# A two-layer kernel on one Trainium2 core: the first step of the forward transforms moves 128 columns (re, im) instead of 192, and the negative real part is made at the evacuation of four images

## Chip, core and metric

The kernel runs on one core of one Trainium2 chip. The metric is the device time of one execution in microseconds (us). Four executions of the kernel before gave 3290.41, 3295.86, 3288.34 and 3288.98 us, median 3289.7 us. The profile shown is of the execution that took 3290.41 us; its span from the first to the last instruction is 3288.7 us, so 1.7 us lie around the span.

Engines are called by their profile names: PE (TensorE, matmuls), PEld (its weight loads), DVE (VectorE), ACT (ScalarE), POOL (GpSimd), SP (SyncE, which here only issues DMAs).

## What is computed

The input is `x` of shape (4, 32, 128, 128) in float32, read as 4 batches of 32 images of 128 x 128. Layer 0 is a Fourier neural operator block with attention; layer 1 is causal attention and a mixture of eight experts over tokens. The change lies in layer 0 alone, and of layer 0 only the forward transforms matter here:

```python
def _spectral_conv(x, w2, oh, ow):
    w = w2[..., 0] + 1j * w2[..., 1]
    X = jnp.fft.rfft2(x, norm='forward')
    Xk = jnp.concatenate([X[:, :, :mh, :mw], X[:, :, -mh:, :mw]], axis=2)
    Yk = jnp.einsum('bixy,ioxy->boxy', Xk, w)
    ...
    return jnp.fft.irfft2(out, s=(oh, ow), norm='forward')
...
xn = _inorm(xa, norm1_w, norm1_b)
k = _fno_layer(xn, Kcw, Ksw, Hs, Ws)          # and q, v: one spectrum of xn serves all three
...                                            # attention over the 32 images, projection p
a = _inorm(p + xa, attn_w, attn_b)
an = _inorm(a, norm2_w, norm2_b)
m = _fno_layer(an, m0cw, m0sw, H, W, inner_norm=True, act=True)
m = _fno_layer(m, m1cw, m1sw, H, W, inner_norm=True, act=False)
out = _inorm(m, mon_w, mon_b) + a
```

Each batch needs three sets of 32 spectra: of the input images (for k, q and v), of the attention's output (first mixer layer) and of its GELU (second mixer layer). Only 64 rows of modes and 33 (or 17) columns of modes are kept, so a truncated transform by two matmuls does it.

## The kernel before

Layer 0 takes the first third of the execution, about 1130 us, layer 1 the rest. Layer 1 has its own hand-written order and is not touched. In layer 0 the program text gives the dependencies and the buffers, and a scheduler with a cost model of its own decides at build time in which order each engine gets its instructions. An edit of an instruction's size can therefore move instructions elsewhere in layer 0; the engines then run their queues strictly in that order.

**The forward transform** (`forward`, L265 to L281) works on groups of eight images (`GI = 8`).

- Step one, L272: for each image one matmul `pz[:, j] = image.T @ rows`. The image is the stationary operand (a 128 x 128 weight load), the constant `rows` is moved. `rows` has 192 columns: cos, -sin, -cos (64 each), so that the result holds the real part, the imaginary part and the negative real part. Two images share one PSUM tile `pz` of 2 x 192 floats; the tag "a" has two such banks, which other stages of layer 0 use as well (the `pv2` of the inverse transforms among them).
- Evacuation, L217 or L219: `evacuate` copies the tile to `z` in SBUF, 128 x 384 floats at once. A counter sends two calls of three to ACT and one to DVE. Four evacuations serve a group.
- Step two, L279 and L280: for each image two matmuls with `z` as stationary operand, accumulating in `px`: `z[:, :128]` (re, im) against the constant `c1`, then `z[:, 64:]` (im, -re) against `c2`. The moved operand has 99 columns (67 for the input images). Four images share a `px` tile; `take` is then called with it.

`forward` is called in three places, each four times per batch (four groups of eight images), 48 times in all:

- `spectra_of_images` (trace name of the moved image: x): `take` is `scaled`, L467 on DVE. Before step two `less_mean` (L472, L473, DVE) subtracts a mean from the first column of the real and of the negative real part of all eight images at once. Its results go out by DMA (`xd`, L485) and come back spread over partitions (`xb`, L696), and they feed `attention_weights` (L526 to L616), where the products `pa` and `pb` (L557 on DVE, L559 on POOL) go into the matmuls of L563.
- `spectra(0, q)`: `take` is `weighted`: a square on ACT (L791), two products on DVE (L792, L795), a sum on POOL (L798). In the same stretch of time DVE does `add_attention` (L768, 32 instructions a batch).
- `spectra(1, gl)` (image: g), likewise; at its end the weights by energy (L808, L812 on DVE, L814 on PE).

So per batch the order of the stages is: values by attention (L711 to L716, L661, L680), inverse transform with L746 and L748, `spectra(0)`, inverse transform with the GELU (L838 to L848), `spectra(1)` and the next batch's `spectra_of_images` side by side, the next batch's `attention_weights`, the last inverse transform (L899). L887 (ACT) and L894 (POOL, 2.4 us each) prepare the last stage and may be placed anywhere between the end of `spectra(1)` and L899. DMAs of SP are issued in order of its queue; in batch 0 this queue holds the two halves of `gd` and `gb` (L515, L517: weights written to DRAM and read back onto all partitions), `xd` and `xb`.

Of the kernel before, what the change touches and what calls it, by code (L numbers as in the profile page):

```python
# [7 lines left out]
F32 = mybir.dt.float32  # L8
AF = mybir.ActivationFunctionType
ALU = mybir.AluOpType  # L10
# [3 lines left out]
P = 128  # L14
# [4 lines left out]
GI = 8  # L19
# [16 lines left out]
def _constants():  # L36

    w = np.arange(P)
    kx = np.concatenate([np.arange(32), np.arange(-32, 0)])
    ky = np.arange(KY)  # L40
    th = 2 * np.pi / P
    c, s = np.cos(th * np.outer(w, kx)), np.sin(th * np.outer(w, kx))
    rows = np.concatenate([c, -s, -c], 1)
    inv_rows = np.concatenate([c.T, -s.T], 0)
    angle = th * np.outer(w, ky)
    cc, cs = np.cos(angle), np.sin(angle)

    cols1 = np.concatenate([cc[:, 32:33], cs, cc, -cs], 1) / NPIX
    cols2 = np.concatenate([0 * cc[:, :1], -cc, cs, cc], 1) / NPIX
    twice = np.where(ky == 0, 1.0, 2.0)[:, None]  # L50
    re, im = twice * cc.T, -twice * cs.T
    inv_cols = np.concatenate([re, im], 0)
    p = np.arange(P)
    same = (p[:, None] % 32 == np.arange(32)[None, :]).astype(np.float64)
    block = (p[:, None] // 32 == np.arange(4)[None, :]).astype(np.float64)

    eye = np.eye(32)
    comb = np.zeros((4, 32, 3, 32))
    comb[0, :, 0], comb[3, :, 0] = eye, -eye
    comb[1, :, 1], comb[2, :, 1] = eye, eye  # L60
    comb[:, :, 2] = -comb[:, :, 0]
    halves = np.concatenate([np.eye(64), np.eye(64)], 0)

    group = (p[:, None] // 4 == p[None, :] // 4) / (4.0 * NPIX / C * T)
    of_group = p[:, None] // 4 == np.arange(32)[None, :]
    by_p = np.concatenate(
        [rows, inv_rows, cols1, cols2, same, block, comb.reshape(P, 96), halves, group, of_group / 4],
        1,
    )
    return by_p.astype(np.float32), inv_cols.astype(np.float32)  # L70


NX = 1 + 3 * KY
NCONST = 192 + 128 + 2 * NX + 32 + 4 + 96 + 64 + P + 32
NM = KX * KY
NK = 13

# [25 lines left out]
def layer0(  # L103
    tc, x, kcw, qcw, vcw, pcw, m0cw, m1cw, mcol0, heads, small_row, by_p, inv_cols, dram, x1
):
    nc = tc.nc
    pools = [tc.tile_pool(name="l0_const", bufs=1), tc.tile_pool(name="l0_ps", bufs=2, space=PSUM)]
    pools.append(tc.tile_pool(name="l0_x", bufs=2))
    const, ps, images = (p.__enter__() for p in pools)
# [17 lines left out]
    def columns(n):  # L127
        at[0] += n
        return cst[:, at[0] - n : at[0]]

    rows = columns(192)
    inv = columns(128)
    cols1, cols2 = columns(NX), columns(NX)
    same, block = columns(32), columns(4)
# [75 lines left out]

    flip = [0]

    def evacuate(out, in_):

        flip[0] = (flip[0] + 1) % 3
        if flip[0]:
            nc.scalar.copy(out, in_)  # L217
        else:
            nc.vector.tensor_copy(out, in_)  # L219

    def per_image(name):
        return small.tile([P, T], F32, name=name, tag=name)
# [41 lines left out]
    def forward(images, c1, c2, take, change=None):  # L264


        n = c1.shape[1]
        z = grp.tile([P, GI, 192], F32, name="z", tag="z")
        for k in range(0, GI, 2):
            pz = ps.tile([P, 2, 192], F32, name="pz", tag="a")  # L270
            for j in range(2):
                nc.tensor.matmul(pz[:, j], images[k + j], rows, start=True, stop=True)  # L272
            evacuate(z[:, k : k + 2], pz)
        if change is not None:
            change(z)
        for k in range(0, GI, 4):
            px = ps.tile([P, 4, n], F32, name="px", tag="b")
            for j in range(4):
                nc.tensor.matmul(px[:, j], z[:, k + j, :P], c1, start=True, stop=False)  # L279
                nc.tensor.matmul(px[:, j], z[:, k + j, 64:], c2, start=False, stop=True)  # L280
            take(k, px)  # L281
# [343 lines left out]
    for b in range(B):  # L625
# [63 lines left out]
        for x0 in range(0, KX, NK):  # L689
# [3 lines left out]
            for i in range(4):  # L693
                xb = late.tile([P, 2, NK * KY], F32, name="xb", tag="xb")[:, :, :m]
                for r in range(2):
                    nc.sync.dma_start(  # L696
                        out=xb[:, r],
# [773 lines left out]
```

## Time and profile before

| part of the profiled execution | value |
|---|---|
| execution, span | 3290.41 us, 3288.7 us |
| ACT, POOL busy over the span | 2356.5 us (72%), 2140.0 us (65%) |
| L272, matmul records | 768 (two for each of 384 matmuls) |
| L279 and L280, matmul records | 768 each |
| L272's time in the 27 us from 473 to 500 us (`spectra(0)`, batch 1) | 12.35 us |
| the same in the 31 us from 558 to 589 us (mostly input images of batch 2) | 12.85 us |
| PE granted clock from 212 us to 327 us, and in the whole span | 1.00, 0.968 |

A float32 matmul of the program is shown as two records, each with its weight load. The time of one record contains its way through the array, so records of neighbouring matmuls overlap; what a matmul costs PE when others follow is the distance from start to start. In the groups, the columns are count, busy time in us, mean of one in ns, and the engine's idle time just before with what ended it. In the chain of waits, time is given to the work that everything after it waited for.

### The profile page before, as it was taken

How to read it: one execution, taken by the hardware profiler on the slowest of the kernel's cores; microseconds unless marked ns; L12 is line 12 of the kernel's file. 1: busy time of each engine (PE TensorE's matmuls, PEld its weight loads, DVE VectorE, ACT ScalarE, POOL GpSimd, SP SyncE). 2: the span in 40 equal slices, each digit the busy share in tenths (PEclk: the TensorE clock that was granted, in tenths of full speed). 3: DMA queues.
4: the chain of work that ended last, by engine and by line, in shares of the span. 5: the costliest groups of instructions: out<-in, count | busy, mean ns of one | idle time of the engine just before them, and what ended most of it. 6: DMA issues, size and time to landing. Idle time of an engine off the chain costs nothing.

```text
span 3288.7 us, 48731 instructions
## 1 busy us (share of the span) xinstructions
PE 3068.0 (93%) x17428; PEld 1494.7 (45%) x17428; DVE 2319.8 (71%) x5070; ACT 2356.5 (72%) x3205; POOL 2140.0 (65%) x1883
## 2 busy tenths in 40 slices
PE   6899899899898699999999999999999999999997
PEld 4378368458558533333333333333333334333333
DVE  6866776767677456777665767766777777677777
ACT  2334344354344289999999999998999999999992
POOL 1731641551460278868788787889877879888773
PEclk8999999999999689999999999999999999999998
DMA  4400410320230111010110000011100010101000
GB/s 108 118 21 5 117 48 1 78 91 1 32 111 1 52 39 26 1 33 7 27 33 20 14 20 14 7 26 26 26 20 14 14 33 20 33 1 26 14 13 13
DMA packets 148274, 107.17 MB, mean 33 GB/s; under 512 B 35358, under 2 KB 138881, under 8 KB 147425
## 3 DMA queue, kind: packets, MB, share of 16 engines
q1 hardware_dynamic: 131313, 98.22, 11.6%
q10 hardware_dynamic: 16720, 5.84, 0.7%
q8 instruction: 138, 2.26, 0.3%
q14 instruction: 103, 0.84, 0.1%
HBM read 67.26 MB, written 20.00 MB: 27 GB/s over the span
## 4 chain that ended last, share of the span: by engine, by line
PE 72%; POOL 10%; DVE 8%; ACT 4%; issue 3%; DMA 2%; ACTq 0%; POOLq 0%; DVEq 0%; SPq 0%
PE d L1282 25%; PE po L1301 13%; PE px L1180 6%; PE po L716 4%; PE pz L272 4%; PE four L294 3%; POOL e L1344 3%; PE pv L289 3%; POOL e L1343 3%; PE px L280 2%; PE px L279 2%; ACT r L1335 2%; PE n L1282 2%; POOL kx L1044 1%; PE sk L680 1%
## 5 line engine op out<-in xcount | busy, mean ns | idle before, releaser
L1282 PE MATMUL d<-qe,ke 32*128 32x512 f32 (+7 forms) x3456 | 1167.6, 603 | 20.8 <-ACT r L1335 20.2
L1340 DVE TENSOR_TENSOR r<-n,r 128x1024 f32<-128x1024 f32 (+1 forms) x1056 | 958.2, 949 | 302.8 <-ACT r L1347 169.5
L1282 PE MATMUL n<-qf,kf 32*128 32x512 f32 (+7 forms) x3456 | 1159.9, 602 | 0.0
L1343 POOL TENSOR_TENSOR e<-r 128x512 f32<-128x512 f32 x528 | 672.8, 1274 | 318.2 <-DVE r L1340 277.6
L1335 ACT ACTIVATE r<-d 128x1024 f32<-128x1024 f32 (+1 forms) x1056 | 822.7, 805 | 70.3 <-PE n L1282 60.0
L1347 ACT ACTIVATE r<-r 128x1536 f32<-128x1536 f32 x528 | 783.4, 1484 | 16.8
L1344 POOL TENSOR_TENSOR e<-e,r 128x512 f32<-128x512 f32 x528 | 672.4, 1273 | 41.4
L1282 PEld LDWEIGHTS d<-qe,ke 32*128 32x128 f32 (+1 forms) x3456 | 352.4, 185 | 701.8 <-issue 243.4
L1301 PE MATMUL po<-e,kx 128*128 128x512 f32 (+3 forms) x1152 | 596.3, 606 | 10.5 <-POOL e L1356 10.5
L1184 DVE SCALAR_TENSOR_TENSOR xc<-px,wgt,xc 128x128 f32<-128x128 f32 x1024 | 358.2, 350 | 212.0 <-PE px L1180 179.4
L1351 ACT ACTIVATE e<-e 128x512 f32<-128x512 f32 x528 | 325.9, 617 | 75.6 <-POOL e L1344 74.9
L1282 PEld LDWEIGHTS n<-qf,kf 32*128 32x128 f32 (+1 forms) x3456 | 350.9, 184 | 19.0 <-DVE r L1340 0.9
L1301 PEld LDWEIGHTS po<-e,kx 128*128 128x128 f32 x1152 | 176.2, 188 | 382.6 <-issue 298.4
L711 POOL TENSOR_TENSOR u<-xb,gb 128x858 f32<-128x858 f32 (+1 forms) x120 | 234.9, 1985 | 117.4 <-PE po L716 106.1
L798 POOL TENSOR_TENSOR spec<-spec,part 128x264 f32<-128x264 f32 x64 | 55.4, 866 | 392.2 <-DVE part L795 188.9
L1180 PE MATMUL px<-we,x2t 128*128 128x512 f32 x512 | 265.9, 605 | 7.0 <-DVE xc L1184 6.2
L713 DVE TENSOR_TENSOR u<-xw,gb 128x858 f32<-128x858 f32 (+1 forms) x200 | 208.5, 1093 | 50.5 <-PE po L716 34.9
L716 PE MATMUL po<-u,pr 128*32 128x429 f32 (+1 forms) x1280 | 187.0, 532 | 19.3 <-POOL u L711 8.7
L705 ACT COPY xw<-xb 128x429 f32<-128x429 f32 (+1 forms) x160 | 83.8, 527 | 127.9 <-DVE pa L557 68.6
L1180 PEld LDWEIGHTS px<-we,x2t 128*128 128x128 f32 x512 | 96.6, 194 | 121.4 <-issue 104.6
L217 ACT COPY z<-pz 128x384 f32<-128x384 f32 x127 | 60.7, 478 | 119.7 <-PE pz L272 119.3
L559 POOL TENSOR_TENSOR pb<-xm 128x1024 f32<-128x1024 f32 x48 | 90.6, 1912 | 83.3 <-ACT xm L493 73.9
(365 smaller groups left out, 3917.6 us busy)
## 6 DMA issues: line engine op xcount, KB each, us to landing
xb<-xd SPq DMA_DIRECT2D x128, 214.5 KB
xc<-x SPq DMA_DIRECT2D x31, 512.0 KB
x<-x SPq DMA_DIRECT2D x16, 512.0 KB
kf<-ks SPq DMA_DIRECT2D x64, 128.0 KB
qf<-qe SPq DMA_DIRECT2D x64, 128.0 KB
out<-xc SPq DMA_DIRECT2D x15, 512.0 KB
xb<-xd SPq DMA_DIRECT2D x32, 198.0 KB
gb<-gd SPq DMA_DIRECT2D x4, 1056.0 KB
```

The lines of the kernel that those rows point to most:

```text
L711: nc.gpsimd.tensor_tensor(u, xb, gk, ALU.mult)
L716: nc.tensor.matmul(po[32 * j : 32 * j + 32], pr[:, i, k], u[:, r], start=i == 0 and k == 0, stop=i == 3 and k == 1,)
L1180: nc.tensor.matmul(px, x2t[:, k * P : (k + 1) * P], we[:, e0 : e0 + 4], start=True, stop=True)
L1184: nc.vector.scalar_tensor_tensor(xc[:, k], px[:, e], wgt[:, k, e0 + e : e0 + e + 1], xc[:, k], ALU.mult, ALU.add)
L1282: nc.tensor.matmul(o, k, q, start=True, stop=True)
L1301: nc.tensor.matmul(sums[c, h][:, q0 : q0 + c1 - c0], kx[:, jb], e[:, c0:c1], start=jb == 0, stop=is_last and q0 > 2 * P, skip_group_check= ...
L1335: nc.scalar.activation(r[:, g], d, AF.Ln, scale=1.0 / DSCALE)
L1340: nc.vector.tensor_tensor(r[:, g], part, r[:, g], ALU.mult)
L1343: nc.gpsimd.tensor_tensor(e, r[:, 0], r[:, 1], ALU.add)
L1344: nc.gpsimd.tensor_tensor(e, e, r[:, 2], ALU.add)
L1347: nc.scalar.activation(r, r, AF.Exp, scale=-1.0)
L1351: nc.scalar.activation(e, e, AF.Exp)
```

## The change

`rows` loses its third block of 64 columns, and L272 moves 128 columns. A `pz` tile now holds four images x 128 columns (one whole PSUM bank) instead of two x 192. For each tile there are two evacuations: re and im of four images (128 x 512 floats), and re again with the factor -1 into the third block of `z` (128 x 256 floats). A group of eight images still has four evacuations and `z` holds the same numbers as before. `evacuate` gets a `sign` and becomes an ACT activation `Copy` with a scale, or a DVE `tensor_scalar` multiply, for all its callers (`v` and `yf` of the inverse transforms too, with 1.0).

```diff
-    rows = np.concatenate([c, -s, -c], 1)
+    rows = np.concatenate([c, -s], 1)
...
-NCONST = 192 + 128 + 2 * NX + 32 + 4 + 96 + 64 + P + 32
+NCONST = 128 + 128 + 2 * NX + 32 + 4 + 96 + 64 + P + 32
...
-    rows = columns(192)
+    rows = columns(128)
...
-    def evacuate(out, in_):
+    def evacuate(out, in_, sign=1.0):
 
         flip[0] = (flip[0] + 1) % 3
         if flip[0]:
-            nc.scalar.copy(out, in_)
+            nc.scalar.activation(out, in_, AF.Copy, scale=sign)
         else:
-            nc.vector.tensor_copy(out, in_)
+            nc.vector.tensor_scalar(out, in_, sign, None, ALU.mult)
...
         z = grp.tile([P, GI, 192], F32, name="z", tag="z")
-        for k in range(0, GI, 2):
-            pz = ps.tile([P, 2, 192], F32, name="pz", tag="a")
-            for j in range(2):
+        for k in range(0, GI, 4):
+            pz = ps.tile([P, 4, P], F32, name="pz", tag="a")
+            for j in range(4):
                 nc.tensor.matmul(pz[:, j], images[k + j], rows, start=True, stop=True)
-            evacuate(z[:, k : k + 2], pz)
+
+            evacuate(z[:, k : k + 4, :P], pz)
+            evacuate(z[:, k : k + 4, P:], pz[:, :, :64], -1.0)
```

The built program, compared with the one before, has the same number of instructions on every engine. The 192 evacuations of `z` are split as before, 127 on ACT and 65 on DVE. Around the forward transforms of layer 0 the scheduler orders instructions of PE, DVE and ACT differently. On POOL ten places differ: among L559 and L894 (the next batch's `pb` and the sums for the last stage). On SP one transfer moves: the second half of `gd` (L515) stands after the two `xd` of batch 0 (L485), and before them in the kernel before. With layer 1 the order begins to be the same again.

## The prediction

> **What bounds the kernel.** I read the page's busy table and slices first, then the chain of waits, then the groups by shape, last the timeline and the chain inside the forward stages.
>
> ```profile
> PE 3068.0 (93%) x17428; PEld 1494.7 (45%) x17428; DVE 2319.8 (71%) x5070; ACT 2356.5 (72%) x3205; POOL 2140.0 (65%) x1883
> PE   6899899899898699999999999999999999999997
> DVE  6866776767677456777665767766777777677777
> PE 72%; POOL 10%; DVE 8%; ACT 4%; issue 3%; DMA 2%; ACTq 0%; POOLq 0%; DVEq 0%; SPq 0%
> ```
>
> PE is the bound in layer 0 (slices 1 to 13 of 82 us) as in layer 1, and holds 72% of the chain. On the page the same chain gives L272 4%, about 130 us. So the changed matmuls lie on the path that sets the end, not beside it. The chain cut to 460 to 600 us confirms it: L272, L279 and L280 follow each other there, and where PE stops it is for an evacuation:
>
> ```profile
> 482.23 1.34 PE pz L272 x8
> 483.59 0.49 ACT z L217
> 484.12 1.57 PE pz L272 x8
> ```
>
> What one matmul costs is its distance to the next. Timeline of PE, three stretches (start, time from first start to last end, count), and one from layer 1:
>
> ```profile
> 49.57 0.39 PE L280 MATMUL px<-colg,z 128*128 128x67 f32 x2
> 49.79 0.39 PE L279 MATMUL px<-colg,z 128*128 128x67 f32 x2
> ...
> 212.72 1.47 PE L272 MATMUL pz<-cst,q 128*128 128x192 f32 x8
> 214.75 1.57 PE L272 MATMUL pz<-cst,q 128*128 128x192 f32 x8 [0.57 <-ACT z L217]
> ...
> 1217.56 0.61 PE L1120 MATMUL pa<-centre,att 128*128 128x129 f32 x4
> ```
>
> L272 with 192 columns: (1.47 - 0.326)/7 = 0.163 us a record (0.326 is its median time). L279 with 67 columns: (49.79 - 49.57)/2 = 0.11 us. L1120 has 129 columns and the same full weight load: (0.61 - 0.275)/3 = 0.112 us. So 67, 99 and 129 columns cost the same 0.112 us: below some 130 columns another limit holds, and 128 columns get no cheaper than that. The 0.57 us in brackets is PE waiting for a `pz` bank.
>
> **What the Trainium skill says.** "TensorE: Matmul & The Clock Gate", section "LDWEIGHTS (loading the stationary operand)", prices a weight load at columns/1.2 ns; for 128 columns that is 107 ns, an estimate from the page. The measured 112 ns agrees, so the floor is the weight load. "VectorE: DVE Perf Modes", section "Why PSUM operands drop a tier", says that float32 from PSUM runs at the lowest rate whatever the operation, so DVE's multiply should cost what its copy did; the trace has no multiply of such a size from PSUM. "PSUM — Partial Sum Buffer", section "PSUM bank collisions raise a hardware error", says that ACT and DVE may not read the same bank at once, reads against reads included. The trace agrees in effect: L791 (ACT) and L792 (DVE) read the same `px`, and L792 waits for L791:
>
> ```profile
> L792 DVE TENSOR_TENSOR spec<-px,mcw 128x264 f32<-128x264 f32 x64 | 27.5, 430 | 40.0 <-ACT sqx L791 38.7
> ```
>
> So the two evacuations of one new `pz` bank run one after the other, on two engines too; the built order of the changed kernel has these waits.
>
> **The change part by part.** Rows used:
>
> ```profile
> L272 PE MATMUL pz<-cst,x 128*128 128x192 f32 x256 | 53.9, 352 | 4.1 <-ACT z L217 3.0 <-DVE z L219 1.0
> L272 PE MATMUL pz<-cst,g 128*128 128x192 f32 x256 | 51.5, 338 | 3.2 <-ACT z L217 1.6 <-DVE z L219 1.6
> L272 PE MATMUL pz<-cst,q 128*128 128x192 f32 x256 | 49.3, 335 | 3.0 <-ACT z L217 2.3 <-DVE z L219 0.6
> L217 ACT COPY z<-pz 128x384 f32<-128x384 f32 x127 | 60.7, 478 | 119.7 <-PE pz L272 119.3
> L219 DVE COPY z<-pz 128x384 f32<-128x384 f32 x65 | 35.8, 550 | 17.2 <-PE pz L272 16.1 <-issue 0.7
> L683 ACT COPY q<-sk 128x512 f32<-128x512 f32 x32 | 18.8, 587 | 39.0 <-PE sk L680 38.8
> L559 POOL TENSOR_TENSOR pb<-xm 128x1024 f32<-128x1024 f32 x12 | 22.7, 1914 | 28.8 <-ACT xm L493 28.0 <-PE sp L563 0.7
> L894 POOL TENSOR_TENSOR x<-x,g 128x1024 f32<-128x1024 f32 x4 | 9.5, 2366 | 0.7 <-DVE pa L557 0.7
> ```
>
> (The last two are of the window 318 to 372 us, POOL alone.)
>
> *Matmuls removed from PE:* 768 records x (0.162 - 0.112) = 38.4 us. Almost all on the path, since PE is 94 to 100% busy in most of the windows of these stages.
>
> *Old stalls removed:* from start to start, 693 pairs of neighbouring L272 records took 26.5 us more than 693 x 0.162; with the steps to and from L279 it is 29 us, 0.6 us for each of the 48 groups of eight. They come from a bank of two images: it fills in 4 x 0.162 = 0.65 us, and its evacuation (0.48 or 0.55 us, plus some 0.16 us until the last matmul has ended and 0.1 us of handover) must be over when the bank after the next is wanted. In the new form a group uses two banks only, each once, so this wait mostly goes.
>
> *New stalls added:* step two of images 0 to 3 now needs both evacuations of the first bank. From rows: ACT costs (587 - 478)/128 = 0.85 ns a float, so 0.59 us for 512 and 0.37 us for 256; DVE, with the 690 ns of L1060's 512-float copy from PSUM, 0.69 and 0.41 us. In series 0.96 to 1.1 us. Timeline for a group: the last matmul of the bank is issued, ends 0.27 us later, handovers 0.1 us, evacuations 1.05 us: `z` is whole 1.42 us after the issue. PE meanwhile fills the second bank (8 x 0.112 = 0.9 us) and does one or two L279 (0.22 us each) that need only the first evacuation; then L280 waits 0.2 to 0.3 us, plus 0.1 us for a weight load that can't be hidden behind it. With DVE evacuations queued behind other DVE work (L768 at 0.35 us, four L748 at 0.87 us together) I take 0.5 us a group, 24 us. Bounds: 0.2 us (10 us), where the scheduler puts other matmuls there (it interleaves two groups in the stage of the input images), and 1.0 us (48 us), where each DVE evacuation waits for a run of L768 or L748. Net of old and new stalls: -5 us; bounds -19 and +19.
>
> *Evacuations:* as many, the same floats, the same split over the engines: ACT 0.59 + 0.37 against 2 x 0.478 us, DVE 0.69 + 0.41 against 2 x 0.55 us. ACT changes from COPY to ACTIVATE; the nearest rows with a fixed scale, L1335 from PSUM, 595 ns for 512 floats, and L683's copy, 587 ns, differ by 1%. I take 0; ends -1 and +2 us over all 288 calls, `v` and `yf` included, most of it off the path.
>
> *`spectra(0)`:* DVE was busy 25.4 of the 28 us from 212 to 240. PE's gain there (3.2 us a batch plus stalls) nearly meets DVE's spare 2.6 us; in the new order several L768 come later, after the stage, from batch 1 on. I charge 1 us a batch for L768 between the steps of the chain from L812 to L838: +4 us (0 to 8).
>
> *POOL in `attention_weights`:* after `xm`, POOL is the bound: 12 L559 x 1.91 + 4 L894 x 2.37 = 32.4 us of the 33.3 us from 327.2 to 360.5. For batch 2 the kernel before runs two L894 ahead of `xm` (584 and 587 us, POOL idle otherwise) and needs 592.1 to 622.8 = 30.7 us. In the new order all four come among the L559, each behind ACT's L887 too: 33.3 us, +2.6 us; for batch 3 three instead of two or so, +1.5 us. Together +4 us (0 to 8).
>
> *SP's queue in batch 0:* the second `gd` was issued at 67.5 us, ahead of the two `xd` (75.3 to 79.9 us, waiting for the last spectra). It now stands behind them, the `gb` that reads it back waits for it, and the `xb` queue up behind `gb`. The chain there runs through them: `xd` 13.2 us, then `xb` 15.9 us to 105 us, and ACT's L705 waits for it. So of batch 0's gain in the stage of the input images (about 4 us) I give back 2 us (0 to 5).
>
> *`NCONST`* is 64 columns smaller: one load at the start, nothing. Layer 1 keeps its order and its clock (PE 1.00 in most of it); its start moves as a whole.
>
> Sum: -38.4 - 5 + 4 + 4 + 2 = -33.4 us. Against the profiled execution (3290.4 us; the median, 3289.7 us, is 0.7 us lower) that is 3257 us.
>
> **Rivals.**
>
> - *Handover dominates:* new stalls 0.8 us a group (38 us), the rest as above with POOL and SP at +10 us: -38.4 + 9 + 10 = -19 us, 3271 us. For it: the two evacuations in series on a shared bank, DVE 90% busy in `spectra(0)`. Against: DVE is only half to two thirds busy in the other two stages.
> - *Stalls nearly vanish:* 0.2 us a group, side costs 2 us: -38.4 - 19 + 2 = -55 us, 3235 us. For it: half as many banks to hand over. Against: the serial reads.
> - *Slower:* one mechanism, the serial pair at the head of each group behind a full DVE queue. Before, a group paid 0.6 us of stalls and 0.8 us (16 x 0.05) for the third block; if L280 waits more than 1.4 us a group (1.2 us with the 10 us of side costs) the change loses. At 1.6 us: 77 - 29 - 38 + 10 = +20 us, 3310 us. It decides only if nearly every group meets a DVE backlog of over 1 us, which the 0.57 us waits of before (one bank behind two L748 runs) show only for the first group of a stage.
> - *No floor below 192:* if 128 columns cost 0.16 us too, little would change; L1120's 0.112 us speaks against it.
>
> **Numbers.** Likeliest 3257 us: chance 0.56, its own range 3245 to 3270. Handover 0.22, stalls vanish 0.11, slower 0.08, nothing left 0.03. A measurement of this kernel tells about 0.2% (6.6 us) from no change: faster by more 0.88, within 0.04, slower 0.08. The range reaches into the two faster-side rivals, to 3234 us (stalls gone) and 3282 us (stalls 1.0 us a group, side costs at 10 us).
>
> **What would show it.** Right: L272 records 0.112 us apart, its group about 40 us less busy; idle before L272 falls, idle before L279 and L280 rises from 1.1 us to about 20 us, released by z on ACT or DVE; the ACT row of z split into 0.59 and 0.37 us; layer 1 unchanged in length. Wrong: L272's distance above 0.13 us; waits of L280 over 1 us in most groups; the stage from `xm` to the last L559 longer by over 5 us in batches 2 and 3; `xb` of batch 0 landing later than 105 us.

## The result, and the profile after

The changed kernel takes 3280.74 us (median of 41 runs, 3271.29 to 3288.64) against 3289.04 us (62 runs on the same chip): ratio 0.997, 95% interval 0.9964 to 0.9977. It is faster, by 8 to 12 us; 33 were forecast. The profiled execution took 3277.85 us (span 3276.1 us, 12.6 us below that of before).

The page of the kernel after, first the busy table, then PE's slices, then the chain of waits by engine:

```profile
PE 3036.1 (93%) x17428; PEld 1461.9 (45%) x17428; DVE 2317.9 (71%) x5070; ACT 2353.3 (72%) x3205; POOL 2139.9 (65%) x1883
...
PE   6699898899898699999999999999999999999997
...
PE 65%; POOL 10%; DVE 6%; ACT 5%; issue 3%; DMA 1%; SPq 0%; POOLq 0%; DVEq 0%; ACTq 0%
```

PE does 32 us less, DVE and ACT the same to 3 us, and the end comes only 12.6 us earlier. PE's second slice (82 to 164 us) fell from 8 to 6 tenths, so a part of what PE saved came back as waiting in batch 0. The groups by shape (busy us, mean ns of one, then idle time before and what ended it):

```profile
L272 PE MATMUL pz<-cst,x 128*128 128x128 f32 x256 | 37.3, 291 | 5.2 <-ACT z L217 5.0
L272 PE MATMUL pz<-cst,g 128*128 128x128 f32 x256 | 36.0, 287 | 0.0
L272 PE MATMUL pz<-cst,q 128*128 128x128 f32 x256 | 31.8, 276 | 0.0
L281 PE MATMUL px<-cst,z 128*128 128x99 f32 x512 | 101.7, 281 | 4.7 <-ACT z L217 2.4 <-DVE z L219 0.9 <-DVE n_r_ve L236 0.5
L217 ACT ACTIVATE z<-pz 128x512 f32<-128x512 f32 x63 | 37.6, 596 | 76.1 <-PE pz L272 74.7 <-issue 1.3
L217 ACT ACTIVATE z<-pz 128x256 f32<-128x256 f32 x64 | 24.3, 379 | 26.5 <-DVE z L219 26.5
L219 DVE TENSOR_SCALAR z<-pz 128x512 f32<-128x512 f32 x33 | 22.5, 682 | 3.8 <-PE pz L272 3.1 <-issue 0.7
```

Lines after L275 stand two lower than before (L279 is L281, L515 is L517, L696 is L698), and lower again in the experiments, which have a helper more. The last three rows show the new serial pair: over all 64 calls, ACT's copy of 256 floats stood 26.5 us for DVE's read of the same bank.

Where did the rest go? The starts of the same steps in both traces show it. In batch 0 the stage of the input images ended 1.2 us earlier than before, but the first L718 (`po`) started at 133.99 us instead of 119.98. When batch 1's first transform starts, the kernel is still 9.2 us late; from there to the last L901 (batches 1 to 3) it gains 21.6 us, and from there to the end both take 2164.8 to 2164.9 us. My sum, split the same way, had 8 us gained in batch 0 and 25.5 in the others: 17 of the missing 21 us of this execution are lost in batch 0.

SP's queue there, kernel before (start, time, issue, count):

```profile
58.04 1.35 SPq L517 DMA_DIRECT2D gb<-gd  x2
67.46 0.33 SPq L515 DMA_DIRECT2D gd<-g  x1
75.25 4.61 SPq L485 DMA_DIRECT2D xd<-xx  x2
80.76 2.33 SPq L517 DMA_DIRECT2D gb<-gd  x2
85.13 23.39 SPq L696 DMA_DIRECT2D xb<-xd  x10
```

and the kernel after:

```profile
61.16 1.36 SPq L519 DMA_DIRECT2D gb<-gd  x2
74.02 8.47 SPq L487 DMA_DIRECT2D xd<-xx  x2
82.58 2.65 SPq L517 DMA_DIRECT2D gd<-g  x1
91.58 1.27 SPq L519 DMA_DIRECT2D gb<-gd  x2
92.96 26.94 SPq L698 DMA_DIRECT2D xb<-xd  x10
```

The second `gd` now goes out 15.1 us later, behind both `xd`. SP stands 6.4 us (85.23 to 91.58) until it has landed, then issues the second pair of `gb`, 10.8 us later than before, and every `xb` is behind it. The first pair of `gb` is late as well, by 3.1 us, and the two `xd` hold SP for 8.47 us instead of 4.61. ACT and DVE in the kernel after show who is caught:

```profile
115.04 0.52 ACT L707 COPY xw<-xb 128x429 f32<-128x429 f32 x1 [38.05 <-DMA xb<-xd]
117.06 0.58 ACT L573 COPY spt<-sp 128x512 f32<-128x512 f32 x1
```

```profile
123.33 0.68 DVE L595 TENSOR_REDUCE mx<-sc 64x16 f32<-64x512 f32 x1 [20.56 <-PE sc L584]
```

`spt` could have run at 104 us, when its last L565 was done. It stands on ACT behind a `xw` that waits for `xb`, and the softmax behind `spt`: DVE waits 20.56 us (5.32 before). This is what the experiments had to test.

### The profile page after: what moved, and what is told of

It reads as the page before. It is cut to its first block, busy times and chain, and to the rows that moved or that the text cites. A ratio compares the mean times of both kernels' runs of the same rounds, so it can differ in the third digit from the quotient of the medians.

```text
span 3276.1 us, 48759 instructions
## 1 busy us (share of the span) xinstructions
PE 3036.1 (93%) x17428; PEld 1461.9 (45%) x17428; DVE 2317.9 (71%) x5070; ACT 2353.3 (72%) x3205; POOL 2139.9 (65%) x1883
## 4 chain that ended last, share of the span: by engine, by line
PE 65%; POOL 10%; DVE 6%; ACT 5%; issue 3%; DMA 1%; SPq 0%; POOLq 0%; DVEq 0%; ACTq 0%
PE d L1284 25%; PE po L1303 13%; PE px L1182 6%; POOL e L1346 3%; POOL e L1345 3%; PE po L718 2%; PE four L296 2%; PE pv L291 2%; PE px L282 2%; PE px L281 2%; ACT r L1337 2%; PE n L1284 2%; POOL kx L1046 2%; PE pz L272 1%; DVE xc L1186 1%
## 5 line engine op out<-in xcount | busy, mean ns | idle before, releaser
L718 PE MATMUL po<-u,pr 128*32 128x429 f32 (+1 forms) x1280 | 185.9, 530 | 19.8 <-POOL u L713 8.7
L561 POOL TENSOR_TENSOR pb<-xm 128x1024 f32<-128x1024 f32 x48 | 90.7, 1915 | 105.6 <-ACT xm L495 97.4
L217 ACT ACTIVATE z<-pz 128x256 f32<-128x256 f32 (+1 forms) x127 | 57.3, 487 | 102.6 <-PE pz L272 74.7
```

The source lines that it names most:

```text
L718: nc.tensor.matmul(po[32 * j : 32 * j + 32], pr[:, i, k], u[:, r], start=i == 0 and k == 0, stop=i == 3 and k == 1,)
```

## The experiments

Each kernel was timed in turns with the kernel before on the same chip; the chips differ, so kernels are compared by their ratio. "Clock" is PE's mean granted clock over the timed runs.

| kernel | ratio, interval | clock | second `gd` | second `gb` | first `po` |
|---|---|---|---|---|---|
| before | 1 | 0.968 to 0.970 | 67.46 | 80.76 | 119.98 |
| after | 0.997 [0.9964, 0.9977] | 0.963 | 82.58 | 91.58 | 133.99 |
| e1 | 0.995 [0.9933, 0.9966] | 0.965 | 71.28 | 83.79 | 127.15 |
| e2 (192 columns) | 1.0023 [1.0013, 1.0032] | 0.969 | 79.64 | 89.38 | 131.63 |
| e3 | 0.9967 [0.9951, 0.9983] | 0.963 | 82.67 | 91.59 | 131.81 |
| e4 | 0.9964 [0.9952, 0.9975] | 0.961 | | | |
| e5 | 0.9932 [0.9908, 0.9955] | 0.964 | 73.11 | 85.24 | 130.77 |
| e6 (192 columns) | 0.9995 [0.9981, 1.0009] | 0.969 | 68.03 | 81.07 | 125.12 |
| e7 | 0.9908 [0.9887, 0.9929] | 0.965 | 72.54 | 84.21 | 122.43 |
| e8 | 0.9947 [0.9931, 0.9962] | 0.965 | 73.60 | 84.64 | 130.31 |
| e9 (192 columns) | 0.9973 [0.9962, 0.9984] | 0.971 | 66.44 | 79.77 | 117.09 |
| e10 (e7 again) | 0.9936 [0.9919, 0.9952] | 0.964 | 72.83 | 84.30 | 122.12 |
| e11 | 0.9918 [0.99, 0.9936] | 0.966 | 70.81 | 85.21 | 120.67 |
| e12 (wide matmuls) | 1.0027 [1.0019, 1.0036] | 0.963 | 69.73 | 83.53 | 121.07 |
| e13 | 0.9924 [0.9907, 0.9941] | 0.966 | 72.04 | 86.47 | 121.44 |
| e14 (192 columns) | 0.9985 [0.9976, 0.9995] | 0.970 | 68.08 | 81.40 | 118.96 |

The edits use one helper that puts an instruction behind another in the planned order, without a semaphore:

```diff
+def behind(tc, later, earlier):
+    tc.add_manual_dep(
+        later.ins,
+        earlier.ins.name,
+        mybir.DependencyInfo(mybir.DependencyClass.NoSync, mybir.DependencyReason.DATA),
+        reason="issue order",
+    )
```

**e1 and e2: SP's order alone, once in each direction.** The changed kernel gets back the place of the second `gd` (ahead of `xd`); the kernel before is given the new one. `marked` holds the two `xd` of each batch, `gds` the `gd`.

```diff
 e1, in the changed kernel
+    for d in marked:
+        behind(tc, d, gds[1])
 e2, in the kernel before
+    behind(tc, gds[1], marked[1])
```

> The changed kernel, with one more order edge: in batch 0 the two xd transfers stand behind the second gd on SP's queue again, as in the kernel before; no other instruction moves on any engine. Theory A (the late second gd, and the gb and xb queued behind it, cost batch 0 about 14 us): the second gd is issued near 67 us, gb near 80 us, po of batch 0 starts near 119 us instead of 134 us, and the time is about 14 us under the changed kernel's, 3267 us, ratio to before 0.993. Rival B (the 15 us before po come from PE's half clock and slower stages; the queue order is incidental): po of batch 0 starts within 3 us of 134 us, ratio 0.997 as for the changed kernel.

> The kernel before, with one more order edge: the second gd of batch 0 stands behind the two xd on SP's queue, as in the changed kernel; nothing else moves. Theory A: gb is issued near 93 us instead of 80.8 us, po of batch 0 starts 12 to 16 us later than 120 us, and the time is 12 to 16 us above before: about 3303 us, ratio 1.004. Rival B: within 3 us of before, ratio 1.000.

SP's queue of e2, the 192-column kernel with one DMA moved:

```profile
75.58 3.96 SPq L495 DMA_DIRECT2D xd<-xx  x2
79.64 2.56 SPq L525 DMA_DIRECT2D gd<-g  x1
89.38 1.27 SPq L527 DMA_DIRECT2D gb<-gd  x2
```

It repeats after's picture: 7 us of standing until `gd` has landed, the first `po` 11.65 us late, 3296.89 against 3288.37 us at the end, 8.5 us by the medians and 0.23% by the ratio. That is less than the 12 to 16 us of theory A, but the order of the DMAs alone costs some 8 us of the end, with no transform changed. e1 gives back about as much (0.2% between the ratios of after and e1, 6.6 us, with intervals that just touch), but only half of the delay of the first `po`. Its trace shows why. The softmax still queues behind `xw`. And the second `gb` still goes out 3 us later than before, though `gd` no longer holds it up: it follows the `xd` at once (73.31 + 10.18 us, then 83.79), and before it was at 80.76 us.

The traces have a regularity here that I had not looked for. In all 16 of them SP is done with the two `xd` 19.6 to 21.4 us after it has issued the last pair of `gb` ahead of them, in e5, e6 and e8 too, where that is the second pair. The first pair goes out at 57.0 to 58.7 us in the kernels with the old transforms and at 61.2 to 64.0 us in those with the new ones, so the new ones are behind at this point already. No run moved this pair alone, so it is not shown that the `xd` wait for it.

**e3: the softmax's first copy ahead of `xw` on ACT**, SP's new order left as it is.

```diff
+                    if len(xws) <= 2:
+                        behind(tc, xws[-1], spts[0])
```

> The changed kernel; in batch 0 alone the first two copies xw (L707, which wait for xb) stand behind the copy spt (L573) on ACT's queue; nothing else moves. Theory A1 (the late xb reaches the end because spt, and the whole softmax behind it, queue behind xw on ACT): sc and the softmax run before xb lands, po of batch 0 starts near 121 us instead of 134 us, 3268 us, ratio 0.993. Rival A2 (the products u need xb anyway, so the late transfer itself is the bound): po starts near 130 us or later, gain of at most 4 us, ratio 0.996 or more.

`spt` moved from 117.06 to 103.37 us and the softmax began 16 us earlier, and nothing was won (ratio 0.9967, as after). DVE of e3:

```profile
107.04 0.68 DVE L605 TENSOR_REDUCE mx<-sc 64x16 f32<-64x512 f32 x1 [5.27 <-PE sc L594]
107.75 0.68 DVE L606 TENSOR_TENSOR ph<-sc,mx 64x512 f32<-64x512 f32 x1
116.75 1.05 DVE L727 TENSOR_TENSOR u<-xw,gb 128x858 f32<-128x858 f32 x1 [8.31 <-ACT xw L717]
117.72 1.00 DVE L609 TENSOR_REDUCE sm<-ph 64x16 f32<-64x512 f32 x1
```

The copy was moved and nothing else of the softmax. Its exponential (L607 on ACT) ran at 116.66 us, behind two `xw` again; its sum (L609 on DVE) then stood behind a `u` that waits for the same `xw`; and `pr`, the probabilities read back, was issued on SP 7.5 us after `prd` (2.5 us in after), which the first `po` awaited for 7.72 us. So theory A1 falls and rival A2 fits: to free one instruction is not enough, since a late `xb` stands ahead of the softmax at several places.

**e5, e6: all three queues, and `gb` too, put ahead.** In both kernels: `gd` and `gb` ahead of `xd`; `xw` behind `spt` (ACT), `u` behind the softmax's last product (DVE), batch 0's later `xb` behind `pr` (SP).

```diff
+    for d in marked[:2]:
+        behind(tc, d, gds[-1])
...
+                    if len(xbs) in (9, 10):
+                        behind(tc, xbs[-1], prs[0])
...
+                            if len(us) <= 4:
+                                behind(tc, us[-1], phs[0])
```

> The changed kernel with order edges in batch 0 alone: both gd and all four gb stand ahead of the two xd on SP; on ACT the first two xw stand behind spt; on DVE the first four products u stand behind the last product of the softmax; on SP the fifth xb tile stands behind the DMA pr. Theory A (batch 0's delay is the queueing of gb, xb and the softmax behind each other, and nothing in the transforms): po of batch 0 starts at 115 to 118 us instead of 134 us, time 15 to 18 us under the changed kernel's: 3264 us, ratio 0.9925. Rival B (the 2.1 MB of gb ahead of xd hold up xd and xb as long as before): xb lands after 112 us, po at 125 us or later, ratio 0.995.

> The kernel before with the same order edges in batch 0. Theory A: the kernel before lost little there, po of batch 0 starts at 116 to 118 us instead of 120 us, ratio 0.999; and the distance of this kernel to the fifth experiment's, with batch 0's queues equal in both, is what the transforms bring alone: 20 to 25 us. Rival: the edges help both kernels alike by over 8 us (ratio under 0.9975), and the distance stays near 8 us.

This overshoots, as rival B had it: `xd` now stands behind `gb` and goes out at 86.6 us instead of 74, `xw` follows at 118.2 us in e5, and the first `po` is no earlier than 130.77 us in e5 and 125.12 us in e6. But the two kernels, with the same edges, are 0.63% apart (0.9932 and 0.9995), 21 us: with the same order of batch 0's queues, the change is worth more than twice what it is as built.

**e7 and e10: `gd` ahead of `xd`, `gb` behind it, and the softmax first**, in the changed kernel (e1's edge with the last three of e5). **e9: the same softmax edges in the kernel before**, whose `gd` already stands ahead.

> As the fifth experiment, but with the second pair of gb left behind the two xd (the order of the kernel before; the second gd ahead of xd). Tells the two edits of the fifth apart. If the softmax's place in the queues is what matters, po of batch 0 starts within 2 us of the fifth experiment's; if gb's place is, xb lands near 108 us, the products u start after the softmax is done and po starts 3 to 8 us later than there (119 to 125 us), ratio 0.994 to 0.995.

> The kernel before with the order edges of e7_after_gd_soft that it did not have already (xw behind spt on ACT, u behind the softmax's last product on DVE, batch 0's later xb behind pr on SP; its second gd already stands ahead of xd). Same work; only these three queues change, in batch 0. Theory A (e7 is 29 us faster than before because the transforms are worth 20 to 25 us once batch 0's queues are put right, and the edges are worth a few us to either kernel): the first po at 115 to 120 us, ratio to before 0.998 to 1.000, and e10_after_gd_soft_2 shorter than this by 20 to 27 us. Rival E (most of e7's gain are the softmax's edges, which have nothing to do with the change): ratio 0.994 or less here, and the two kernels 10 us or less apart.

> e7_after_gd_soft once more, on the chip and beside the runs of before that e9 and e11 have. Ratio to before 0.989 to 0.993, if its first figure (0.9908 from 6 runs) holds.

e7 came out at 0.9908 and its repeat at 0.9936, a little above the 0.989 to 0.993 that I expected: on two chips this version is some 21 to 29 us faster than the kernel before, and faster than after. Its first `po` comes 8.3 us earlier than e5's, where I had expected the same or later, so `gb` behind `xd` is the better place. Its SP queue is in the order of before again:

```profile
72.54 0.33 SPq L527 DMA_DIRECT2D gd<-g  x1
74.56 9.36 SPq L497 DMA_DIRECT2D xd<-xx  x2
84.21 3.83 SPq L529 DMA_DIRECT2D gb<-gd  x2
90.76 20.60 SPq L710 DMA_DIRECT2D xb<-xd  x8
```

But e9 takes away a part of the claim that went with it. The softmax edges are worth 0.27% (9 us) to the kernel before as well, where I had allowed 0.2% at most. On e9's chip the changed kernel is then 0.37% ahead (13 us, by the medians 3282.78 and 3269.40), less than the 20 to 27 us expected of theory A, more than the rival's 10. The change, with batch 0's queues put right in both kernels, is worth 13 us in this pair and 21 in e5 and e6, not 33 to 35.

The same order does not make batch 0 equal. Batch 1's first transform starts 7.4 us later in e10 than in e9, and 4.3 us later in e5 than in e6; from there to the end of layer 0 e10 gains 20.0 us and e5 16.5 us. In both pairs the new form is behind at the first `gb` already, by 4.9 and 3.6 us.

**e11: one pair on DVE.** In after and e7, DVE stands 3.7 to 4 us (in e1 2.8 us) for a `px` of PE with the last sum of the second `g` behind it. One edge lets the sum (L526) go first.

```diff
+    behind(tc, xxs[6], adds[1])
```

> e7 with one more edge: batch 0's seventh L469 (xx, evacuation of px) stands behind the second L516 (the sum that completes the second g) on DVE. One pair of DVE instructions changes places, nothing else. In e7 DVE stood 3.73 us before that L469, waiting for PE, with the finished operands of the second g queued behind it. Theory A in full (the second g is late only by its place in DVE's queue, and what follows it in batch 0 follows its landing): g is whole at 68 instead of 72.5 us, the second gd is issued at 68 to 69, the first po starts 3 to 4 us earlier (118 to 119.5), the time is 2 to 4 us below e10. Rival F (xd's packets, not the second gd, set when gb and xb land): gd earlier by 3.5 us, but xw and po move by less than 1 us, time within 1 us of e10.

DVE of e10's kernel, in its first run e7, and of e11:

```profile
66.99 0.17 DVE L240 TENSOR_TENSOR sel<-cst,n_s 128x32 f32<-128x32 f32 x1
70.89 0.44 DVE L479 TENSOR_TENSOR xx<-px,n_s 128x268 f32<-128x268 f32 x1 [3.73 <-PE px L292]
71.24 1.27 DVE L526 TENSOR_TENSOR g<-g,t 32x1088 f32<-32x1088 f32 x1
```

```profile
68.36 0.17 DVE L240 TENSOR_TENSOR sel<-cst,n_s 128x32 f32<-128x32 f32 x1
69.51 1.28 DVE L526 TENSOR_TENSOR g<-g,t 32x1088 f32<-32x1088 f32 x1 [0.97 <-ACT g L522]
70.80 0.44 DVE L479 TENSOR_TENSOR xx<-px,n_s 128x268 f32<-128x268 f32 x1
```

`g` was done 1.7 us earlier and no more, since ACT's L522 had been the next to come late. The first `po` started 1.5 us earlier, half of what theory A said, and the time (6 us by the ratios, with intervals that overlap) can't be told from e10's. Nor did the gain come by the way that theory A gave: the second `gb` went out later, not earlier (85.21 us, 84.30 in e10), right behind an `xd` that was done later. So the run decides between neither. This is the fastest version of its chip, with e10.

**e4 and e8: the serial pair at the head of a group.** e4 is e1 with the negative part made from `z` in SBUF, so that nothing reads a bank twice (the scheduler reorders layer 0 for it). e8 is e5 with the last L272 of each group made twice, 48 matmuls more, meant to fill PE while it waits for `z`.

```diff
 e4
-            evacuate(z[:, k : k + 4, P:], pz[:, :, :64], -1.0)
+            evacuate(z[:, k : k + 4, P:], z[:, k : k + 4, :64], -1.0)
 e8
+                if k + j == GI - 1:
+                    nc.tensor.matmul(pz[:, j], images[k + j], rows, start=True, stop=True)
```

> The first experiment's kernel, with the negative real part made from the real part in z (SBUF) instead of from the pz bank; the bank is then free after one evacuation, and the order of the two evacuations stays, since the second reads what the first wrote. The scheduler orders layer 0 anew. Theory S (of the waits inside the forward transforms, about 10 us are for a bank whose two reads run in series, some 20 us for z): the waits between neighbouring L272 fall from about 10 us to under 4 us, the waits before the matmuls on z stay within 5 us of 21 us, and the time is 3 to 8 us under the first experiment's. Rival T (the reads in series don't matter; the waits are queueing behind other work on DVE and ACT): the waits between L272 fall by less than 3 us and the time is within 3 us of the first experiment's.

> The fifth experiment's kernel; the last matmul of step one of every group of eight is made twice (48 matmuls more, the same numbers, 48 x 0.224 = 10.8 us of PE work, and all of layer 0 ordered anew by the scheduler). Theory C (PE waits for z some 0.34 us a group, and these gaps bring PE's clock to half): the work fills the gaps, waits before the matmuls on z fall from 16 us to 6 to 10 us, neighbouring records of the transforms at half clock fall from 64 or more to under 40, and the time is within 4 us of the fifth experiment's. Rival D (the gaps have nothing to do with the clock): half-clock records stay at 60 or more and the time rises by 5 to 10 us.

ACT of e4 against the rows above: the second part from SBUF is dearer, and ACT's wait for DVE no shorter.

```profile
L227 ACT ACTIVATE z<-z 128x256 f32<-128x256 f32 x64 | 26.6, 415 | 30.0 <-DVE z L229 29.0
```

From the distances of neighbouring records, the waits before step two fell from 16 us in e1 to 9 in e4, and those between L272 stayed (7.3 and 8.0 us at full clock), so theory S had it the wrong way round. All distances in the transforms sum to 9 us less in e4 (277.7 and 286.8 us), yet it is not faster: 0.9964 against 0.995, with intervals that overlap. Its order of layer 0 is another and its clock is lower (0.961), so e4 does not show what these waits cost.

e8 did not fill the gaps. Its waits before step two are still some 15 us (16 in e5), 5.4 us of them right behind a doubled matmul. The time is 7.6 us above e5's for 10.8 us of added matmuls (96 records of 0.112 us), and 74 records of the transforms run at half clock (111 in e5; theory C said under 40). Rival D's numbers came true, but with the gaps left open the run does not test theory C.

**e12: wide matmuls in the changed kernel.** The table has a pattern that no theory of queues explains. Kernels with the old transforms (before, e2, e6, e9, e14) have a mean clock of 0.968 to 0.971, those with the new ones 0.961 to 0.966, whatever the order in batch 0. e12 is e7 with three of four L272 widened to 192 columns; the 64 extra columns land in the area of the image before, which the next matmul overwrites.

```diff
-            for j in range(4):
-                nc.tensor.matmul(pz[:, j], images[k + j], rows, start=True, stop=True)
+            flat = pz.rearrange("p j c -> p (j c)")
+            for j in (3, 2, 1, 0):
+                lead = 64 if j else 0
+                nc.tensor.matmul(
+                    flat[:, P * j - lead : P * j + P],
+                    images[k + j],
+                    rows[:, 64 - lead :],
+                    start=True,
+                    stop=True,
+                )
```

> e7/e10 with wide matmuls: three of the four L272 of a bank move 192 columns again (the block of the negative real part goes ahead and lands in the area of the image before, which the next matmul overwrites; the images are taken in the order 3, 2, 1, 0). Banks, evacuations, z and results are those of e7; the planner moves instructions of layer 0 about, since these matmuls are dearer to it. Added PE time: 576 records x 0.050 = 29 us. What is asked is where the lower mean clock of the changed kernels comes from (0.964 to 0.966 in e5, e7, e10, e11 against 0.969 to 0.971 in e6 and e9, the same orders with the 192-column transforms; by the records 126 to 139 us of PE busy at half clock between 42 and 1130 us against 91 and 92). Theory H (it comes with the shorter matmuls): mean clock 0.968 or more, PE busy at half clock below 105 us, and the time 29 us less 6 to 17 above that of e7/e10, 12 to 23 us: ratio 0.996 to 0.999. Rival I (it comes with the larger bank and its two evacuations in series, the waits before L281): mean clock 0.963 to 0.966, PE busy at half clock 120 us or more, and the whole 29 us: ratio 1.000 to 1.002.

The clock stayed at 0.963 (22 runs; 0.969 in the 27 of before beside them), so the lower clock does not come with the shorter matmuls, and theory H falls. It comes with something else in the new form, the bank of four with its evacuations or the order that the scheduler makes of them; e12's order differs from e7's in layer 0, so these two stay together.

The time rose by 0.9 to 1.2% above e10 and e7, 30 to 39 us, a little more than rival I gave. It is no measure of the columns, though: the distances in the transforms grew by 8 to 14 us (303.8 us; 296.0 in e10, 290.3 in e7), and e12 is ahead of both when batch 2's first transform starts (551.8 us; 559.6 and 558.3). It loses 38 to 43 us after that, with another order.

**e13 and e14: one wait of PE in batch 0.** In all ten kernels with the new form up to e12 a stretch of half clock begins at 66 to 72 us, inside the transforms, and lasts 13.6 to 17.1 us; in before, e2, e6 and e9 it begins at 76 to 80 us, after them, and lasts 3.4 to 6.8 us. PE and DVE of after show what stands ahead of it:

```profile
62.38 1.11 PE L272 MATMUL pz<-cst,x 128*128 128x128 f32 x8
66.20 1.12 PE L281 MATMUL px<-colg,z 128*128 128x67 f32 x4 [2.72 <-DVE z L474]
67.12 0.63 PE L282 MATMUL px<-colg,z 128*128 128x67 f32 x2
67.55 0.63 PE L281 MATMUL px<-colg,z 128*128 128x67 f32 x2
```

```profile
62.94 1.27 DVE L514 TENSOR_TENSOR t<-pw,v 32x1088 f32<-32x1088 f32 x1
64.13 0.67 DVE L219 TENSOR_SCALAR z<-pz 128x512 f32<-128x512 f32 x1
64.73 1.27 DVE L515 TENSOR_TENSOR t<-t,t 32x1088 f32<-32x1088 f32 x1
65.93 0.22 DVE L474 TENSOR_SCALAR z<-z,m 128x8 f32<-128x8 f32 x1
```

The evacuation of `z` stands behind L514, the subtraction of the mean behind L515, and PE waits 2.72 us. It is the backlog of my rival for slower, at one group. Two pairs of records then are 0.43 us apart (67.12 to 67.55) where they were 0.22: half clock. e13 puts L514's product behind the subtractions in e7's kernel; e14 makes a wait in e9's.

```diff
 e13
+    behind(tc, prods[1], means[3])
 e14
+    behind(tc, means[2], adds[1])
```

> e7/e10 with one edge on DVE in batch 0: the second L526 product (t from pw and v, 1.27 us) stands behind the last group's evacuation of z and both subtractions of the mean, with the sum after it (another 1.27 us) behind them too. Ten lines of DVE's order change, no other engine's. In e7 and e10 PE waits some 2.7 us there for z, and its clock is half from 67.2 us on for 17 us. Theory G (that wait of PE brings the half clock of batch 0, which makes px, g and xd's stage late): PE waits 1.5 us or less, no half-clock stretch begins between 64 and 74 us, the input images' stage ends 3 us or more earlier, the second gd goes out at 68 to 70 us, the first po at 117 to 120, and the time is 3 to 6 us below e7/e10: ratio 0.990 to 0.991 (0.9922 is their mean). Rival K (the half clock there has another origin in the new form): the stretch begins at 66 to 72 us all the same and lasts 13 us or more; the time within 2 us of e7/e10.

> The reverse in e9 (192 columns): the third group's first subtraction of the mean stands behind the last sum of the second g on DVE, 2 to 3 us later than in e9 (63.5 us); the planner also moves a few of the last group's matmuls ahead on PE, which fill part of the wait. In e9 the half-clock stretch of this place begins at 76.3 us, after the transforms, and lasts 6.8 us. Theory G, if the wait left on PE is 2 us or more: a half-clock stretch begins between 64 and 74 us and lasts over 7 us, and the first po comes 2 us or more later than e9's 117.1. Rival K: the stretch begins at 74 to 80 us as in the other kernels of the old form.

PE of e13 at the same group:

```profile
64.33 1.11 PE L282 MATMUL pz<-cst,x 128*128 128x128 f32 x8
66.56 0.66 PE L291 MATMUL px<-colg,z 128*128 128x67 f32 x4 [1.12 <-DVE z L484]
67.06 0.39 PE L292 MATMUL px<-colg,z 128*128 128x67 f32 x2
67.28 0.39 PE L291 MATMUL px<-colg,z 128*128 128x67 f32 x2
```

With the wait at 1.12 us the matmuls go on 0.22 us apart; the half clock begins at 73.4 us, behind the transforms, and lasts 6.8 us. `xm` ends 2.8 us earlier than in e10. So in this order it is this wait that brings the half clock of batch 0 (theory G, for this place). A single long wait is not needed: in e12, PE waits 0.96, 1.22 and 0.60 us there, and the half clock begins at 71.8 us all the same. The time did not follow: 0.9924, as e7 and e10 in the mean. The second `gd` went out 0.5 to 0.8 us earlier (72.04 us), but the second `gb` 2.2 us later than in e10 (86.47 us), behind an `xd` that held SP for 13.31 us, and `xw` came at 110.4 us, 1.1 earlier: the DMAs are late next. e14 decides nothing: the scheduler put the last group's matmuls into the wait, which left three of 0.43 to 0.65 us, and the half clock began behind the transforms (79.5 us), as in e9.

## Why the prediction was wrong

Three steps failed, and none of them makes up the miss of some 24 us alone: SP's queue, the net of the stalls, and a granted clock that I had put at nothing.

**"SP's queue in batch 0", 2 us (0 to 5): failed, 7 to 8.5 us.** I saw the move: the second `gd` behind the two `xd`, `gb` waiting for it, `xb` behind `gb`. I priced only a part of batch 0's gain. What I left out first was the length of `gd`'s way once it is queued there: it is issued when the `xd` are through (82.58 us), SP then stands 6.4 us for its landing, and from the second `gb` to the first `xw` pass another 23.5 us (23.3 before), so that all of it goes on to `xw`. And I named ACT's L705 as waiting without asking what is queued behind it: `spt`, and behind that the softmax. The first `po` is 14 us late instead of 2 early. At the end, 7 to 8.5 us of this are the order of the DMAs alone (e1 on the changed kernel, e2 on the one before), where I had charged 2. The rest of batch 0's delay is the softmax behind `xw` (its edges gave the kernel before 9 us too, e9) and a `gb` that is 3 us late from the start. My own list of what would prove it wrong had this sign, `xb` of batch 0 landing after 105 us; it landed at 115.

**Matmuls, -38.4 us: right.** L272's median distance is 0.112 us (0.163 before). 128 columns reach the floor that 67, 99 and 129 had shown, and don't go below it. That the weight load makes this floor was argued from a figure near it; no run tested it.

**Net of old and new stalls, -5 us: failed, about +5.** At full clock, new stalls before L281 and L282 are 16.6 us and what is left before L272 is 7.7, together 24.3, where I had taken 24. But the old stalls were not 29 us: 24.6 at full clock and 2.2 of half clock. And the transforms' records that run at half clock rose from 12 to 64, at 0.11 us extra each, 7.2 us. All distances in the transforms sum to 284.9 us (317.9 before): 33 us gained, not 43.

**Evacuations, 0: right.** ACT 0.596 and 0.379 us, DVE 0.682 and 0.416 (estimated 0.59, 0.37, 0.69, 0.41). That two engines may not read one bank at once, as the Trainium skill has it ("PSUM — Partial Sum Buffer", "PSUM bank collisions raise a hardware error"), agrees with the trace: the two readers go in series, and ACT stood 26.5 us behind DVE. In e4 the wait is the same, since the second part then needs the first one's `z`.

**POOL in `attention_weights`, +4 us: about right.** From `xm` to the last L561 the stage grew by 4.6 us in batch 2, by 0.8 in batch 1, and shrank by 2.5 in batch 3 (batch 0: no change): +2.9.

**`spectra(0)`, +4 us: about right.** From the stage's first L272 to the first L840, the sum that the GELU takes, the four batches gained 1.65, 2.0, 2.8 and 1.3 us, 7.8 together. A third of the transforms' measured 33 us is 11, so 3 are missing.

**Not in the sum at all: the granted clock.** I took the speed of PE as given. (The 1.00 in the table of before leaves out 3.41 us of half clock at 242 us; from 212 to 327 us the mean is 0.985.) From 42 us to the end of layer 0, PE was busy at half clock for 100 us before and 117 after; in the pairs of equal order for 90 and 119 (e6, e5) and 83 and 122 (e9, e10). A record at half clock takes twice its time, so half of the difference is lost to PE, 8, 14 and 20 us, of which 5 in the first pair are the stalls' half-clock share above. (The figures in e12's expectation run to 1130 us. By then the faster kernels are in layer 1, where the first stretch of half clock lasts 47.8 us in most traces, old form or new, so they overstate the difference.) Windows of the two kernels in batch 0 and later (length, PE and its count, the other engines, clock granted to PE, DMA share, GB/s), before and after:

```profile
42.00:150.00 108.00, 91.44 (x664) 50.27 (x662) 82.04 (x123) 31.83 (x62) 50.36 (x26) 0.89 0.42 102
560.00:825.00 265.00, 241.67 (x1968) 172.07 (x1967) 189.76 (x445) 108.70 (x242) 102.97 (x62) 0.95 0.21 53
```

```profile
42.00:150.00 108.00, 78.09 (x519) 43.05 (x518) 71.34 (x114) 22.69 (x43) 38.28 (x20) 0.76 0.42 86
560.00:825.00 265.00, 236.37 (x2017) 166.72 (x2016) 192.20 (x452) 108.92 (x247) 104.46 (x64) 0.94 0.20 53
```

In batch 0 the low figure is partly harmless (PE waits for `xb` then) and partly the stretch that e13 took out of the transforms. In this pair that is nearly all: from 150 us on, PE was busy at half clock for 83 us before and 86 after. In the other two pairs the later batches have 20 and 29 us more.

What it costs there can be read from 13 traces, since from batch 1 on the five kernels with the old transforms have one order of DVE, ACT and POOL, and the eight traces of after, e1, e3, e5, e7, e10, e11 and e13 another. From batch 1's first transform to the end of layer 0 the old form took 817 to 827 us (mean 822.5) with 63 to 80 us of PE busy at half clock, the new one 800 to 814 us (mean 806.0) with 73 to 100. Within each group a trace with more half clock is longer, by 0.56 and 0.44 us for each us (correlation 0.93 and 0.88), near the half that was reckoned. So batches 1 to 3 gain 16.5 us in the mean, and at equal half clock (78 us) an estimated 24, close to the 25.5 of my sum. A wait of PE could lengthen the stretch and lower the clock alike, so this fits the cost but is no proof of it.

The account of the profiled pair: transforms -33, other PE work at half clock +3, POOL +3, `spectra(0)` +3, the DMA order +8: -16, against -12.6 in the spans. The terms overlap in batch 0, and single traces of one order differ by 10 us and more from batch 1 on, so this says that the sizes fit roughly, not that any term of 3 us is sure.

**What stays open.** What lowers the clock in the other batches. The Trainium skill ("TensorE: Matmul & The Clock Gate", "A second HAM failure mode: psum-queue depth-cycling") describes PE going idle briefly between groups of matmuls that cycle through PSUM banks, and the clock falling for it. In batch 0 the wait that e13 shortened and e12's three short ones agree with it. For the later batches the traces speak against it: in after and e10 only one of the 17 and 18 stretches of half clock that begin after 150 us begins between two matmuls of a forward transform, and most begin in `attention_weights` or in an inverse transform. Not tried: a bank of two images with 128 columns, e12 in e7's exact order, and the new form with its first `gb` as early as before. No run gave the clock of all batches back with the rest unchanged.

## What to carry to other kernels

When a change moves a DMA past another on its queue, follow it to its landing and from there to the last instruction that waits for it, and then read every queue in which a waiter stands: what is behind the waiter waits too, and freeing one instruction (e3) only shows the next. Judge such a change with the same order around both versions: as built it was worth 9 us, with the queues set alike in both 13 to 21, and the order edges another 16 to the changed kernel (0.997 to 0.9922, the mean of e7 and e10). And what is saved on PE can be lost again to its clock: compare PE's busy time at half clock in both traces, up to the same point of the program and not to the same microsecond.

## What the runs showed of the hardware that was not expected

- PE's half-clock stretches last 3.41 us or a multiple (10.24 and 17.07 us in the changed kernel's batch 0), as the Trainium skill ("TensorE: Matmul & The Clock Gate", "What's actually happening") says of its window. Two forms of the same transforms got a mean clock 0.005 apart, over dozens of runs on four chips.
- The same DMAs held SP for very different times. The two `xd`, the same bytes each time, took 4.61 us in the kernel before, 8.47 in after, 10.18 in e1 and 20.06 in e5; in all 16 traces their issue was over 19.6 to 21.4 us after that of the pair of `gb` ahead of them (2 x 1056 KB).
- Half clock came behind a PE wait of 2.72 us (after), but also behind three waits of 0.96, 1.22 and 0.60 us (e12), and not behind one of 1.12 us (e13).
- The negative copy of 256 floats from SBUF takes ACT 415 ns, from PSUM 379 ns.
